# Axial attention: values and embeddings summed into one PSUM tile of 32-row strips

## Chip, cores and metric

The kernel runs on one core of one Trainium2 chip. The metric is the device time of a whole execution in microseconds (us). The kernel before takes 5311.62 us as the median of three runs (5309.52 to 5312.31).

## What is computed

The program is four residual layers on an image `x` of 2 x 128 x 128 x 128 (batch, channels, height, width), all in float32: an axial attention, four directional scans, a deformable convolution and a transformed convolution. Only the first layer is touched:

```python
x = x + L0(group_norm(x))
# L0: for every image n, column w and group g of 8, over the 128 rows h
q, k (8 x 128), v (16 x 128) = batch_norm(w_qkv applied to x)
qr = einsum('bgci,cij->bgij', q, q_emb)
kr = einsum('bgci,cij->bgij', k, k_emb).swapaxes(2, 3)
qk = einsum('bgci,bgcj->bgij', q, k)
sim = softmax(sum of batch_norm([qk, qr, kr]), axis=3)
sv  = einsum('bgij,bgcj->bgci', sim, v)        # the values
sve = einsum('bgij,cij->bgci', sim, v_emb)     # the embeddings
out = batch_norm(concat([sv, sve])) summed over the two
```

The last batch norm needs the mean and variance of every channel of `sv` and of `sve` over all images and columns.

## The kernel before

`layer0_prepare` writes the scaled q and k (scratch tensors `qa`, `qb`) and the values (`v`) to DRAM. `layer0_attention` (from line 615) does the rest, and `Merge` (line 931) reads `sv` and `sve` back, normalises them with the statistics and adds them to the image.

**Units and pairs.** Line 669 lists 64 units: image `n`, then group `g`, then a block `wc` of 32 columns. A unit has four *pairs* of 8 columns each, so there are 256 pairs. The loop at line 867 runs over pairs `m`, and then 15 rounds more to drain. The engines are wrapped in `InOrder` (line 75): every engine executes its instructions in the order in which the loop writes them, so this order is the schedule. Line 83 is the helper's line, and nearly everything in the profile bears it; groups are told apart by their tiles.

**One round m**, in order:

1. `logits_pe` (line 726): 8 transposes of the position term `r` and 8 small products of q and k add up in the PSUM tile `lg`; `add_term` (VectorE) adds the other term into `e`.
2. `turn`/`turned` for pair m-2: TensorE transposes half of the finished `e` into PSUM `te`, VectorE copies it to `et`.
3. `maxima` of pair m (VectorE), `divide` of pair m-1 (VectorE's reciprocal of `total`, then POOL's multiplication of `e`).
4. `values` for pair m-3 (line 804): 8 products `et` x `v` into `po`, each into 16 rows of one of four 32-row strips; ScalarE copies `po` to `svt`.
5. `terms_pe` for the next unit: 16 products into the PSUM tile `gen`; `terms_copy`: three quarters by ScalarE, one quarter by VectorE, into `r`.
6. `embedded_pe` for piece m-7 (line 819): 32 products `et2` x `ve`, again into 16 rows of four strips of the same `po`; ScalarE copies `po` to `ste`.
7. the second half of the transposes, then POOL's `by_position`, which rearranges `et` into `et2`; last the 8 `exponentials` of pair m on ScalarE, with their sums.
8. `stats` (line 848, called from line 906): one `bn_stats` over 512 elements for each half unit of `svt` and of `ste`, so four per unit; a `bn_aggr` when a group is complete.
9. the loads on SyncE's queue (SP) for units to come: 16 of `zz` and one of `vt` (line 684, three buffers), four of `qk`; then the stores of `svt` and `ste`, four each.

Both products use the one PSUM tile `po` (line 657), one after the other, with a ScalarE copy after each. Each float32 product shows in the profile as two records of weight load and matmul, a transpose as one.

At the start of the attention the table `ve` is loaded by ScalarE's queue (line 650) and `zz` is cleared by POOL (line 655). At the end, `Merge.scales` (line 970) gathers the statistics with one small matmul (line 982) through a constant matrix `gather` (line 2107).

Of the kernel before, what the change touches and what calls it, by code (L numbers as in the profile page):

```python
# [7 lines left out]
F32 = mybir.dt.float32  # L8
I32 = mybir.dt.int32
AF = mybir.ActivationFunctionType  # L10
ALU = mybir.AluOpType
# [4 lines left out]
P = 128  # L16
N = 2
S = 128
RT = 4
NT = S // RT  # L20
WC = 32
NC = S // WC
NB = S // 16
NG = 8
# [589 lines left out]
def layer0_attention(env, prm, mem, alphas, mv, then):  # L614
# [14 lines left out]
    nc, tc = env.nc, env.tc  # L629
    pe, dve, act, pool, sync = (  # L630
        InOrder(tc, e) for e in (nc.tensor, nc.vector, nc.scalar, nc.gpsimd, nc.sync)
    )
    ident = env.ident
    HW = WC // 2
    with ExitStack() as ctx:
        early = ctx.enter_context(ExitStack())
        cp = ctx.enter_context(tc.tile_pool(name="at_c", bufs=1))
# [7 lines left out]
        st_v, st_e = (  # L645
            cp.tile([P, NG, N * NC, 2, 6], F32, name=f"st_so{k}", tag=f"st_so{k}")
            for k in range(2)
        )
# [25 lines left out]
        def load(at):  # L674
            u = Unit()
            u.n, u.g, u.wc = units[at]
            u.z = zz[at % 2]
            u.base = 64 * (at % 2)
            for i in range(16):
                sync.dma_start(  # L680
                    out=u.z[8 * i : 8 * i + 8, :, i % 4].rearrange("p t b w -> p t (b w)"),
                    in_=qb[u.g, u.n, u.wc, i],
                )
            u.v = sp.tile([P, WC, 16], F32, name="vt", tag="vt", bufs=3)
            sync.dma_start(out=u.v, in_=mem["v"][u.g, u.n, u.wc])
            u.r = {}
            return u

# [115 lines left out]
        def values(u, p, et):  # L804

            for r in range(2):
                for x in range(RT):
                    pe.matmul(
                        po_v[32 * x : 32 * x + 16, r, :],
                        lhsT=u.v[:, (2 * p + r) * RT + x, :],  # L810
                        rhs=et[:, r * RT + x, :],
                        start=True,
                        stop=True,
                    )
            if p == 0:
                u.sv = sp.tile([P, 2 * RT, S], F32, name="svt", tag="svt")
            act.copy(u.sv[:, 2 * p : 2 * p + 2, :], po_v)

        def embedded_pe(u, k):
# [12 lines left out]
        def embedded_copy(u, k):  # L832
            if k == 0:
                u.sve = sp.tile([P, WC, WC], F32, name="ste", tag="ste")
            act.copy(u.sve[:, 8 * k : 8 * k + 8, :], po_e)

        def store_sv(u):
            for x in range(4):
                sync.dma_start(out=sv[u.g, x, :, u.n, u.wc], in_=u.sv[32 * x : 32 * x + 16])

        def store_sve(u):
            for s in range(4):
                sync.dma_start(
                    out=sve[u.g, s, :, u.n, u.wc],
                    in_=u.sve[32 * s : 32 * s + 16].rearrange("p i w -> p (i w)"),
                )

        def stats(u, st, t, half):
            dve.bn_stats(
                st[:, u.g, u.n * NC + u.wc, half, :],  # L850
                t.rearrange("p a b -> p (a b)")[:, 512 * half : 512 * half + 512],
            )

        pairs = 4 * len(units)
        us, es, ets, totals = {}, {}, {}, {}
        for at in range(2):
            us[at] = load(at)  # L860
            load_qk(us[at])
        for t in range(2):
            for k in range(2):
                ps = terms_pe(us[0], t, k)
                for s in (0, 1):
                    terms_copy(us[0], t, k, ps, s)
        for m in range(pairs + 15):
            here = m < pairs
            if m == pairs:
                early.close()  # L870
# [24 lines left out]
            if 0 <= piece < pairs:  # L895
                embedded_pe(us[piece // 4], piece % 4)
                embedded_copy(us[piece // 4], piece % 4)
            if turning:
                te = turn(e, 1)
                turned(et, 1, te)  # L900
                by_position(ub, pb, et)
                ets[m - 2] = et
            if here:
                totals[m] = exponentials(es[m], mx)

            for st, k, half in ((st_v, 7, 0), (st_v, 8, 1), (st_e, 11, 0), (st_e, 14, 1)):
                if m >= k and (m - k) % 4 == 0 and (m - k) // 4 < len(units):
                    done = us[(m - k) // 4]
                    stats(done, st, done.sv if st is st_v else done.sve, half)
                    if half == 1 and done.n == N - 1 and done.wc == NC - 1:  # L910
                        k = int(st is st_e)
                        every = st[:, done.g].rearrange("p e f k -> p (e f k)")
                        dve.bn_aggr(mv[:, done.g, k, :], every)
# [4 lines left out]
            if m % 4 == 3 and m >= 7 and (m - 7) // 4 < len(units):  # L918
                store_sv(us[(m - 7) // 4])
            if m % 4 == 3 and m >= 11 and (m - 11) // 4 < len(units):  # L920
                store_sve(us[(m - 11) // 4])
            if m % 4 == 2 and m >= 14 and (m - 14) // 4 < len(units):
                us.pop((m - 14) // 4)

# [6 lines left out]
class Merge:  # L931
# [38 lines left out]
    def scales(self, cp, pp, prm, mv):  # L970
# [5 lines left out]
        gather = cp.tile([P, P + NG], F32, name="gather", tag="gather")  # L976
        nc.scalar.dma_start(out=gather, in_=prm["cst"][:, 8 * P : 9 * P + NG])
# [4 lines left out]
        nc.tensor.matmul(  # L982
            ps.rearrange("p g k -> p (g k)"),
            lhsT=gather[:, 0:P],
            rhs=mv.rearrange("p g k m -> p (g k m)"),
            start=True,
            stop=True,
        )
        own = cp.tile([P, NG, 4], F32, name="own", tag="own")
        nc.vector.tensor_tensor(  # L990
            own, ps, gather[:, P : P + NG].unsqueeze(2).to_broadcast([P, NG, 4]), ALU.mult
        )
        gm = cp.tile([P, 2, 2], F32, name="gm_out", tag="gm_out")
        nc.vector.tensor_reduce(
# [1097 lines left out]
def constants(np):  # L2092

    k, m = np.arange(P)[:, None], np.arange(P)[None, :]
    ident = k == m
# [8 lines left out]
    ones = k >= 0 * m  # L2104


    gather = (k % 32 == m % 16) * 0.25
    own = k // 16 == m
    parts = [ident, group_avg, strip, *sel, *selv, ones, gather, own]
# [110 lines left out]
```

## Time and profile before

| what | value |
|---|---|
| median of 3 runs | 5311.62 us |
| profiled execution | 5305.85 us |
| its span | 5304.1 us |
| TensorE busy (matmuls, whole span) | 4974.9 us, 94% |
| VectorE, ScalarE, POOL busy | 3521.7, 2658.8, 2126.1 us |
| first gen matmul of the attention | 402.9 us |
| last copy of po | 1923.9 us |
| `svt<-po` copies on ScalarE | 256, median 0.358 us |
| `ste<-po` copies on ScalarE | 256, median 0.364 us |
| `po<-et,vt` and `po<-et,ve` matmul records | 4096 and 16384 |
| DMA packets, mean rate | 499988, 66 GB/s |

A row of the timeline gives the start, the time from the first start to the last end, the engine, the line, the operation with its tiles (written <- read), the shapes and how many instructions are merged. PE is TensorE's matmuls, PEld its weight loads, DVE VectorE, ACT ScalarE, SP the queue of SyncE. A bracket says how long the engine was idle before, and what ended it. Matmuls are pipelined, so the start of one group to the start of the next is a better measure than the duration. In a list of waits the numbers are the total in us, how many, and the longest.

### The profile page before, as it was taken

How to read it: one execution, taken by the hardware profiler on the slowest of the kernel's cores; microseconds unless marked ns; L12 is line 12 of the kernel's file. 1: busy time of each engine (PE TensorE's matmuls, PEld its weight loads, DVE VectorE, ACT ScalarE, POOL GpSimd, SP SyncE). 2: the span in 40 equal slices, each digit the busy share in tenths (PEclk: the TensorE clock that was granted, in tenths of full speed). 3: DMA queues.
4: the chain of work that ended last, by engine and by line, in shares of the span. 5: the costliest groups of instructions: out<-in, count | busy, mean ns of one | idle time of the engine just before them, and what ended most of it. 6: DMA issues, size and time to landing. Idle time of an engine off the chain costs nothing. (4 is left out here: it accounts for less than half of the span.)

```text
span 5304.1 us, 179050 instructions
## 1 busy us (share of the span) xinstructions
PE 4974.9 (94%) x76283; PEld 4306.7 (81%) x76283; DVE 3521.7 (66%) x6818; ACT 2658.8 (50%) x7718; POOL 2126.1 (40%) x1749
## 2 busy tenths in 40 slices
PE   7898999999999934999999999999989999999999
PEld 6767888888888834999999999998468888888777
DVE  3636888888888857555555555666346666666688
ACT  3557898888889845554222332001334443443322
POOL 3214666666666634000000000333035555555576
PEclk8998999999999966999999999999989999999999
DMA  4362333333333369970000000101321111111011
GB/s 160 122 252 63 62 62 61 58 61 62 59 59 63 61 258 305 92 65 2 1 1 1 1 1 1 49 33 38 117 69 35 35 33 38 33 33 32 35 53 57
DMA packets 499988, 347.61 MB, mean 66 GB/s; under 512 B 311669, under 2 KB 456565, under 8 KB 487281
## 3 DMA queue, kind: packets, MB, share of 16 engines
q1 hardware_dynamic: 494144, 326.50, 27.0%
q8 instruction: 607, 9.95, 0.8%
q10 hardware_dynamic: 5040, 9.56, 0.5%
q14 instruction: 197, 1.61, 0.1%
HBM read 194.99 MB, written 157.72 MB: 66 GB/s over the span
## 5 line engine op out<-in xcount | busy, mean ns | idle before, releaser
L83 PE MATMUL pl<-ln,wl 128*128 128x128 f32 (+1 forms) x10160 | 1241.2, 276 | 9.3 <-DVE ln L83 7.8
L83 PEld LDWEIGHTS pl<-ln,wl 128*128 128x128 f32 x10160 | 1176.1, 190 | 22.3 <-issue 6.7
L83 POOL TENSOR_TENSOR w<-d 128x504 f32<-128x504 f32 x512 | 558.6, 1115 | 669.4 <-DVE s L83 612.8
L83 ACT ACTIVATE e<-e,mx 128x128 f32<-128x128 f32 x2048 | 793.4, 395 | 0.8 <-DVE mx L83 0.8
L83 POOL TENSOR_TENSOR res<-ln,x1t 128x128 f32<-128x128 f32 x256 | 149.3, 584 | 1428.2 <-DVE ln L83 1428.2
L83 POOL TENSOR_TENSOR e<-e,total 128x1024 f32<-128x1024 f32 x256 | 485.9, 1898 | 486.4 <-DVE total L83 477.1
L83 ACT COPY res<-ln 128x64 f32<-128x64 f32 (+1 forms) x1016 | 283.9, 304 | 702.2 <-DVE ln L83 702.2
L83 ACT COPY sm<-ps_s 128x1152 f32<-128x1152 f32 x256 | 286.6, 1119 | 562.6 <-PE ps_s L83 562.6
L83 PE MATMUL po<-sm,wdef 128*128 128x256 f32 x2304 | 567.5, 392 | 0.0
L83 PEld LDWEIGHTS ps_s<-s,xw 28*128 28x128 f32 x10240 | 456.6, 187 | 122.2 <-issue 77.2
L83 PE MATMUL pl<-ln,ws 128*128 128x128 f32 x4064 | 536.8, 273 | 0.0
L83 PE MATMUL ps_s<-s,xw 28*128 28x240 f32 (+2 forms) x10240 | 520.0, 343 | 16.4 <-DMA xw<-px_d 13.9
L83 POOL COPY et<-et 128x1024 f32<-128x1024 f32 x256 | 516.4, 2017 | 35.2 <-DVE et L83 27.0
L83 DVE TENSOR_TENSOR v<-pl,c 128x128 f32<-128x128 f32 x508 | 148.1, 291 | 540.7 <-PE pl L83 537.4
L83 PEld LDWEIGHTS pl<-ln,ws 128*128 128x128 f32 x4064 | 494.5, 190 | 0.0
L83 ACT ACTIVATE r<-gen,alphas 128x1536 f32<-128x1536 f32 x256 | 395.0, 1543 | 170.6 <-PE gen L83 143.6
L83 PEld LDWEIGHTS po<-sm,wdef 128*128 128x128 f32 x2304 | 418.4, 190 | 71.0 <-issue 0.2
L83 ACT ACTIVATION_READ_ACCUMULATOR e<-e,mx 128x1 f32 x2048 | 396.5, 194 | 0.0
L83 DVE SCALAR_TENSOR_TENSOR ln<-v,res 128x128 f32<-128x128 f32 x1016 | 347.0, 342 | 48.5 <-POOL res L83 0.9
L83 DVE STREAM_TRANSPOSE s<-w 128x1152 f32<-128x1152 f32 x256 | 349.8, 1367 | 33.0 <-PE ps_s L83 29.9
L83 PE MATMUL te<-cst_main,e 128*128 128x128 f32 x2048 | 338.5, 287 | 28.7 <-POOL e L83 20.9
L83 DVE COPY et<-te 128x512 f32<-128x512 f32 x512 | 348.2, 680 | 12.9 <-PE te L83 12.4
(246 smaller groups left out, 8405.5 us busy)
## 6 DMA issues: line engine op xcount, KB each, us to landing
xw<-px_d SPq DMA_DIRECT2D x528, 56.0 KB
xa<-in_x SPq DMA_DIRECT2D x16, 1024.0 KB
v_d<-vs SPq DMA_DIRECT2D x16, 1024.0 KB
qb_d<-sb SPq DMA_DIRECT2D x16, 1024.0 KB
qa_d<-sa SPq DMA_DIRECT2D x8, 2048.0 KB
zz<-qb_d SPq DMA_DIRECT2D x1024, 16.0 KB
vt<-v_d SPq DMA_DIRECT2D x64, 256.0 KB
qk<-qa_d SPq DMA_DIRECT2D x256, 64.0 KB
```

Source lines behind the costliest of these rows:

```text
L83: return lambda *a, **k: self.tc.keep_in_program_order(issue(*a, **k))
```

## The change

`values` and `embedded_pe` no longer write `po` one after the other; they add into it. Each strip of 32 rows holds the values of pair m-3 in rows 0 to 15 and the embeddings of piece m-7, which belongs to the unit before, in rows 16 to 31. For this the weights are 32 columns wide: `vt` is now three fixed tiles with zeros in the upper 16 columns (set once), and `ve` has zeros in the lower 16. The values start the sum, the embeddings add onto it (in the last rounds, where there are no values, the embeddings start it). One ScalarE copy `both_copy` takes `po` to a tile `so`, and one `bn_stats` per half unit covers both, so two per unit.

The units are ordered by group first, so that the eight entries of a group lie one after the other in the statistics, values at entry b and embeddings at entry b+1. The stores take rows 0 to 15 and 16 to 31 of each strip of `so` and alternate between `sv` and `sve`. The loop drains in 8 rounds. The constant `gather` has two matrices, and `scales` two matmuls.

```diff
-        ve = cp.tile([P, S, 16], F32, name="ve", tag="ve")
-        nc.scalar.dma_start(out=ve, in_=prm["vemb"])
+        ve = cp.tile([P, S, 32], F32, name="ve", tag="ve")
+        nc.gpsimd.memset(ve[:, :, 0:16], 0.0)
+        nc.scalar.dma_start(out=ve[:, :, 16:32], in_=prm["vemb"])
+        vt = [cp.tile([P, WC, 32], F32, name=f"vt{j}", tag=f"vt{j}") for j in range(3)]
+        for t in vt:
+            nc.gpsimd.memset(t[:, :, 16:32], 0.0)
...
-        units = [(n, g, wc) for n in range(N) for g in range(NG) for wc in range(NC)]
+        units = [(n, g, wc) for g in range(NG) for n in range(N) for wc in range(NC)]
...
-            u.v = sp.tile([P, WC, 16], F32, name="vt", tag="vt", bufs=3)
-            sync.dma_start(out=u.v, in_=mem["v"][u.g, u.n, u.wc])
+            u.v = vt[at % 3]
+            sync.dma_start(out=u.v[:, :, 0:16], in_=mem["v"][u.g, u.n, u.wc])
...
-                        po_v[32 * x : 32 * x + 16, r, :],
+                        po_v[32 * x : 32 * x + 32, r, :],
                         lhsT=u.v[:, (2 * p + r) * RT + x, :],
                         rhs=et[:, r * RT + x, :],
-                        start=True,
-                        stop=True,
+                        start=(r == 0),
+                        stop=False,
...
-            act.copy(u.sv[:, 2 * p : 2 * p + 2, :], po_v)
...
-                        po_e[32 * s : 32 * s + 16, i % 8, :],
+                        po_e[32 * s : 32 * s + 32, i % 8, :],
                         lhsT=ve[:, at, :],
                         rhs=u.et[:, at, :],
-                        start=True,
-                        stop=True,
+                        start=(alone and i % 8 == 0),
+                        stop=(i % 8 == 7),
...
-            act.copy(u.sve[:, 8 * k : 8 * k + 8, :], po_e)
+        def both_copy(b, k):
+
+            if k == 0:
+                sos[b] = sp.tile([P, 4, 256], F32, name="so", tag="so")
+            act.copy(sos[b][:, k, :], po)
...
-        for m in range(pairs + 15):
+        for m in range(pairs + 8):
...
-            for st, k, half in ((st_v, 7, 0), (st_v, 8, 1), (st_e, 11, 0), (st_e, 14, 1)):
+            for k, half in ((5, 0), (7, 1)):
...
-        nc.tensor.matmul(
-            ps.rearrange("p g k -> p (g k)"),
-            lhsT=gather[:, 0:P],
...
+        for k in range(2):
+            nc.tensor.matmul(
+                ps[:, :, 2 * k : 2 * k + 2],
+                lhsT=gather[:, k * P : (k + 1) * P],
```

More of the change, by code (lines that the diff above doesn't have):

```diff
@@ L643, in layer0_attention @@
         pp = ctx.enter_context(tc.tile_pool(name="at_ps", bufs=1, space=PSUM))
[L645 to L648, printed above, removed]
-        ve = cp.tile([P, S, 16], F32, name="ve", tag="ve")
-        nc.scalar.dma_start(out=ve, in_=prm["vemb"])
+        st = cp.tile([P, NG * N * NC + 1, 2, 6], F32, name="st_so", tag="st_so")
+        ve = cp.tile([P, S, 32], F32, name="ve", tag="ve")
[4 more added lines that the diff above has]
+            nc.gpsimd.memset(t[:, :, 16:32], 0.0)
         toep = zp.tile([P, 2, 8, S], F32, name="toep", tag="toep")
@@ L808, in values, with embedded_pe @@
                     pe.matmul(
-                        po_v[32 * x : 32 * x + 16, r, :],
+                        po_v[32 * x : 32 * x + 32, r, :],
                         lhsT=u.v[:, (2 * p + r) * RT + x, :],
                         rhs=et[:, r * RT + x, :],
-                        start=True,
-                        stop=True,
-                    )
-            if p == 0:
-                u.sv = sp.tile([P, 2 * RT, S], F32, name="svt", tag="svt")
-            act.copy(u.sv[:, 2 * p : 2 * p + 2, :], po_v)
-        def embedded_pe(u, k):
+                        start=(r == 0),
+                        stop=False,
+                        skip_group_check=True,
+                    )
+        def embedded_pe(u, k, alone):
             for i in range(8 * k, 8 * k + 8):
@@ L824, in embedded_pe @@
                     pe.matmul(
-                        po_e[32 * s : 32 * s + 16, i % 8, :],
+                        po_e[32 * s : 32 * s + 32, i % 8, :],
                         lhsT=ve[:, at, :],
                         rhs=u.et[:, at, :],
-                        start=True,
-                        stop=True,
+                        start=(alone and i % 8 == 0),
+                        stop=(i % 8 == 7),
+                        skip_group_check=True,
                     )
-        def embedded_copy(u, k):
+        def both_copy(b, k):
@@ L833, in embedded_copy, with store @@
             if k == 0:
-                u.sve = sp.tile([P, WC, WC], F32, name="ste", tag="ste")
-            act.copy(u.sve[:, 8 * k : 8 * k + 8, :], po_e)
-        def store_sv(u):
+                sos[b] = sp.tile([P, 4, 256], F32, name="so", tag="so")
+            act.copy(sos[b][:, k, :], po)
+        def store(b, so):
             for x in range(4):
[L839 to L846, printed above, removed]
@@ L848, in stats @@
-        def stats(u, st, t, half):
+                if b < len(units):
+                    u = us[b]
+                    sync.dma_start(
+                        out=sv[u.g, x, :, u.n, u.wc],
+                        in_=so[32 * x : 32 * x + 16].rearrange("p k (r h) -> p (k r) h", r=2),
+                    )
+                if b > 0:
+                    u = us[b - 1]
+                    sync.dma_start(
+                        out=sve[u.g, x, :, u.n, u.wc],
+                        in_=so[32 * x + 16 : 32 * x + 32].rearrange("p k i -> p (k i)"),
+                    )
@@ L849, in stats @@
+        def stats(b, half):
             dve.bn_stats(
-                st[:, u.g, u.n * NC + u.wc, half, :],
-                t.rearrange("p a b -> p (a b)")[:, 512 * half : 512 * half + 512],
-            )
+                st[:, b, half, :],
+                sos[b].rearrange("p k i -> p (k i)")[:, 512 * half : 512 * half + 512],
+            )
+            per = N * NC
+            for k in range(2):
+                g, rest = divmod(b + 1 - k, per)
+                if half == 1 and rest == 0 and g > 0:
+                    g -= 1
+                    every = st[:, per * g + k : per * g + k + per]
+                    dve.bn_aggr(mv[:, g, k, :], every.rearrange("p e f k -> p (e f k)"))
@@ L857, in layer0_attention @@
         pairs = 4 * len(units)
-        us, es, ets, totals = {}, {}, {}, {}
+        us, es, ets, totals, sos = {}, {}, {}, {}, {}
         for at in range(2):
@@ L895, in layer0_attention @@
             if 0 <= piece < pairs:
-                embedded_pe(us[piece // 4], piece % 4)
-                embedded_copy(us[piece // 4], piece % 4)
+                embedded_pe(us[piece // 4], piece % 4, m - 3 >= pairs)
+            if m >= 3:
+                both_copy((m - 3) // 4, (m - 3) % 4)
             if turning:
@@ L904, in layer0_attention @@
                 totals[m] = exponentials(es[m], mx)
-            for st, k, half in ((st_v, 7, 0), (st_v, 8, 1), (st_e, 11, 0), (st_e, 14, 1)):
[L907 to L913, printed above, removed]
+            for k, half in ((5, 0), (7, 1)):
+                if m >= k and (m - k) % 4 == 0:
+                    stats((m - k) // 4, half)
             if m % 4 == 3 and m // 4 + 2 < len(units):
@@ L917, in layer0_attention @@
                 load_qk(us[m // 4 + 1])
[L918 to L921, printed above, removed]
+            if m % 4 == 3 and m >= 7:
+                store((m - 7) // 4, sos.pop((m - 7) // 4))
             if m % 4 == 2 and m >= 14 and (m - 14) // 4 < len(units):
@@ L975, in scales @@
         nc.scalar.dma_start(out=vec, in_=prm["vecout"])
-        gather = cp.tile([P, P + NG], F32, name="gather", tag="gather")
-        nc.scalar.dma_start(out=gather, in_=prm["cst"][:, 8 * P : 9 * P + NG])
+        gather = cp.tile([P, 2 * P + NG], F32, name="gather", tag="gather")
+        nc.scalar.dma_start(out=gather, in_=prm["cst"][:, 8 * P : 10 * P + NG])
         sq = cp.tile([P, NG, 2], F32, name="sq_out", tag="sq_out")
@@ L981, in scales @@
         ps = pp.tile([P, NG, 4], F32, name="ps_mv", tag="ps_mv")
-        nc.tensor.matmul(
-            ps.rearrange("p g k -> p (g k)"),
-            lhsT=gather[:, 0:P],
[L985 to L988, printed above, removed]
+        for k in range(2):
+            nc.tensor.matmul(
+                ps[:, :, 2 * k : 2 * k + 2],
+                lhsT=gather[:, k * P : (k + 1) * P],
+                rhs=mv[:, :, k, :],
+                start=True,
+                stop=True,
+            )
         own = cp.tile([P, NG, 4], F32, name="own", tag="own")
         nc.vector.tensor_tensor(
-            own, ps, gather[:, P : P + NG].unsqueeze(2).to_broadcast([P, NG, 4]), ALU.mult
+            own, ps, gather[:, 2 * P : 2 * P + NG].unsqueeze(2).to_broadcast([P, NG, 4]), ALU.mult
         )
@@ L2104, in constants @@
     ones = k >= 0 * m
-    gather = (k % 32 == m % 16) * 0.25
+    gather = [(k % 32 == 16 * t + m % 16) * 0.25 for t in range(2)]
     own = k // 16 == m
-    parts = [ident, group_avg, strip, *sel, *selv, ones, gather, own]
+    parts = [ident, group_avg, strip, *sel, *selv, ones, *gather, own]
     cst = np.concatenate([np.broadcast_to(a, (P, P)).astype(np.float32) for a in parts], 1)
```

## The prediction

> **What bounds the kernel now.** The change touches the attention, which runs from about 403 us to 1925 us of the span, so I asked first who is short of time there, with the busy times of three equal stretches, then for the order of TensorE's work in one pair, then for what TensorE waited for.
>
> ```profile
> core 0: us, PE busy (x) PEld busy (x) DVE busy (x) ACT busy (x) POOL busy (x), PEclk, DMA share, GB/s
> 940.00:1400.00 460.00, 445.55 (x11398) 374.74 (x11396) 394.74 (x560) 410.44 (x1511) 309.63 (x160) 1.00 0.33 61
> ```
>
> TensorE 97%, ScalarE 89%, VectorE 86%, clock 1.00. A busy matmul row is weak evidence, so one pair in order of time:
>
> ```profile
> 1263.30 1.04 PE L83 MATMUL lg<-cst_main,r 128*128 128x128 f32 x8
> 1264.27 1.16 PE L83 MATMUL lg<-qk 8*128 8x128 f32 x16
> 1265.36 0.66 PE L83 MATMUL te<-cst_main,e 128*128 128x128 f32 x4
> 1265.94 0.63 PE L83 MATMUL po<-et,vt 128*16 128x128 f32 x16
> 1266.51 1.17 PE L83 MATMUL gen<-zz,toep 32*128 32x128 f32 x32
> 1267.61 0.73 PE L83 MATMUL po<-et,ve 128*16 128x32 f32 x64
> 1268.27 0.66 PE L83 MATMUL te<-cst_main,e 128*128 128x128 f32 x4
> 1268.76 1.04 PE L83 MATMUL lg<-cst_main,r 128*128 128x128 f32 x8
> ```
>
> From lg to lg is 5.46 us with no idle mark: each group starts where the previous one runs out. Seven groups, from start to start: 0.97 + 1.09 + 0.58 + 0.57 + 1.10 + 0.66 + 0.49 = 5.46. Four pairs make a unit: 21.84 us. The starts of the maxima on VectorE give 23.07 us per unit (from unit 4 to unit 60, 1,292 us over 56). So 1.23 us per unit is TensorE time lost. The waits of its weight loads between 480 and 1860 us name it:
>
> ```profile
> PEld po L83 <- issue: 61.3, 267, 1.4
> PEld gen L83 <- issue: 48.2, 228, 0.2
> PEld te L83 <- POOL e L83: 25.8, 84, 0.7
> PEld te L83 <- issue: 5.6, 16, 1.1
> PEld te L83 <- DVE total L83: 2.3, 2, 1.2
> ```
>
> "Issue" is mostly the normal 0.12 to 0.2 us at each change of group, plus stalls inside a group: the first gen of a unit is some 0.39 us longer (its loads carry the waits on 16 loads of zz), and about one embedded group in eight stops for 0.3 to 1.2 us. The change leaves both. What it can give back is the wait of the transposes te for POOL and VectorE: 25.8 + 2.3 = 28.1 us in 86 waits, of which 0.12 us each is the normal step: 86 × 0.12 = 10.3. Real wait: **17.8 us**. ScalarE, meanwhile, waits 134 us for gen there: it has time to spare.
>
> **The change, part by part.**
>
> **ScalarE.** Per pair one COPY po of 0.36 us goes (256 in all, 92 us busy). On the path it is worth nothing: behind it r waits for gen (0.3 to 0.8 us in nearly every pair), and that wait only grows.
>
> **VectorE.** Four BATCH_NORM_STATS2 of 0.68 us per unit (0.60 from start to start) become two. Where do they decide? A statistic stands ahead of the next pair's sum, copy, maxima and reciprocal; the reciprocal releases POOL's division (1.90 us), which releases te one pair later. From VectorE's r at 1252.30 over two statistics to its r two pairs on, at 1263.86, that chain takes 11.56 us; with one statistic that is 10.96, with none 10.36, against 2 × 5.46 = 10.92 us of TensorE. So one statistic per pair is level with TensorE, two are late. Before, pairs 0 and 2 of a unit end with one, pair 3 with two. The te waits, measured from the end of the qk group to te, fit: about 0.10 us in pair 0, 0.15 in pair 1, 0.04 in pair 2, 0.01 in pair 3 (sum 0.30 per unit). After, pairs 1 and 3 end with one each. Pair 1's wait loses 0.60 us of cause and goes, those of pairs 0 and 2 go; a wait like pair 0's (0 to 0.10) moves to pair 3. The 16 BATCH_NORM_AGGREGATE (0.59) stay 16. Gain between 11.6 us (it moves whole) and 17.8 (all goes). I take **−15**, because TensorE itself becomes a little slower (next part) and so hides more of it.
>
> **TensorE, wider weights.** Every weight load of po goes from 16 columns to 32: 64 records per pair in embedded, 16 in values. Nothing covers this engine, so it counts in full. No row has this operand, but one is near: pg in the stage before, 64 loads of 32 columns in the same four strips.
>
> ```profile
> L83 PEld LDWEIGHTS po<-et,ve x16384: 92/96/132, 466.9 to 1923.6; 128*16 128x16 f32 x200
> L83 PE MATMUL po<-et,ve x16384: 189/193/242, 466.9 to 1923.6; 128*16 128x32 f32 x200
> L83 PEld LDWEIGHTS pg<-zt x2048: 105/109/116, 244.4 to 386.8; 128*32 128x32 f32 x187
> L83 PE MATMUL pg<-zt x2048: 192/197/218, 244.4 to 386.8; 128*32 128x33 f32 x187
> 383.29 0.77 PE L83 MATMUL pg<-zt 128*32 128x33 f32 x64
> ```
>
> One load is 13 ns longer, but the whole group only 0.77 against 0.73 us, a part of that from 33 moving columns in place of 32 (32/33 of 0.77 is 0.75). The Trainium skill (TensorE: Matmul & The Clock Gate, LDWEIGHTS) speaks against this change: load time is the number of columns over 1.2, so 16 more cost 13.3 ns each. The 13 ns in the rows agree; as a sum, an estimate from that page, 64 × 13.3 = 0.85 us per pair or 215 us over 253 pairs. By the group row it is 0 to 0.04, since a load in one strip runs beside matmuls in the others. The row decides: 0.025 per pair. Values stream 128 columns per load: 0. Start and stop flags, and adding onto what lies in po, cost nothing in the lg group, which does the same.
>
> **TensorE, waits.** The first embedded matmul no longer waits for ScalarE. The compiled order shows what comes instead: the last three transposes of the first te carry a wait for ScalarE each (the exponentials two pairs back, long done). In layer 1, weight loads with a satisfied wait are followed by their matmul 111 to 112 ns after the last one, unmarked transposes 109: 3 × 3 ns; as bound 3 × 0.03, the price per wait in the first gen. I take 0.01. Together 0.035 per pair × 253 = **+9** (0 to +30).
>
> **DMA.** The target of vt now lies in pieces of 64 B: 4,096 per unit where there were 128 of 2 KB. The nearest row is x1c_d in layer 1, also 64 B: 32,768 pieces take SP 25.6 us, 1,280 per us, so 3.2 us per unit. The skill (DMA: Bandwidth & Descriptors, Specifications) asks for 512 B and more, below that it sees a read-modify-write; no run here shows one for SBUF, so up to twice that, 6.4 us. Behind vt on SP stand the stores, then qk and zz of later units. SP idles about 8 us ahead of every vt (in one unit from 1027.9 to 1035.9), qk and zz are needed some four pairs later, the DMA share of 0.33 rises to 0.47. Price 0. What is exposed if the cover fails: TensorE's own program arrives by DMA in 16 KB packets of about 1.23 us here, and of about 1.4 in the flood of x1c_d. A unit fetches some four, one in five would meet the flood, and 0.2 us on that one is under 0.2 us per unit even if all of it stalls, while one group in eight stalls now; I take **+1** (0 to +20). The stores keep size and number; values and embeddings alternate and the first copy of an output tile waits for all eight, issued three pairs earlier: 0. The order of units changes which loads come, not how many.
>
> **Start.** Four POOL memsets (16 and 3 × 4 KB) are new; zz's 128x2048 takes 1.81 us, so 4 to 8 us in a POOL that idles 43 us until 433.6. The first vt waits for them on SP, ahead of qk and zz of unit 1. Before, it left at 405.66, 13 us after ve could be loaded. ve in 16,384 pieces takes 12.8 us beside zz's last loads; r on ScalarE comes 17 us after its issue. **+1** (0 to +6).
>
> **Drain.** In the last pairs nothing overlaps: po by values, svt, then embedded 0.49 us after it. Twice that step (0.37 + 0.49, less the 0.2 of a group change) goes: −1.3. The last embedded copy stays last; scales has one small matmul more (0.3). **−1**.
>
> **Sum.** −15 + 9 + 1 + 1 − 1 = −5. The profiled execution was 5305.85 (span 5304.1), 5.8 under the median of 5311.62; its sum gives about 5301, that of the median about 5306.5. I say 5306.
>
> **Rivals.** *Wide loads exposed (slower).* Break-even: 17.8 + 1 us over 253 × 64 = 16,192 loads is 1.2 ns per load. Were strips less independent than in pg, 2 ns per load would be +32 − 15 = +17: 5329. For it: TensorE has no slack. Against: pg shows at most 0.6 ns. 0.18.
> *Fetches late.* The 64 B pieces delay TensorE's program; 0.3 us more stall per unit is +19 over 63 units, 5325. For it: stalls are there already. Against: layer 1's TensorE keeps 99.8% busy through a heavier flood, if with fewer instructions. 0.10, and 0.05 for the start or an aggregate going wrong, near 5324.
> *All te waits go and the wide loads are free.* −17.8 − 1 + 1: 5294. For it: pg's surplus may be its wider operand. 0.22.
> *It only moves waits* belongs to my case: gain 11.6, cost 9, 5309.
>
> **Numbers.** Mine 0.45, with 5299 to 5313. What cannot be told from no change is 0.2%, 10.6 us, so 5301.0 to 5322.2. Faster: 0.08 of mine + 0.20 of the free case = 0.28. Same: 0.37 + 0.02 + 0.01 = 0.40. Slower: 0.17 + 0.10 + 0.05 = 0.32. The range 5294 to 5330 leaves out the tails.
>
> **What will show it.** po<-et,ve ×64 in the timeline at 0.73 to 0.77 us; te waits for POOL under 6 us in all and in pair 3; ScalarE's wait for gen longer by 0.36 per pair; vt's issue near 3 us with no TensorE wait behind it; the unit at 22.9 to 23.0 us. An embedded group of 0.80 or more, or more issue stalls in po, would make the prediction wrong.

## The result, and the profile after

The changed kernel takes **5335.52 us** (median of 8 runs, 5323.03 to 5349.58) against 5311.97 us of the kernel before beside it (8 runs, 5305.67 to 5315.69): ratio 1.0044, 95% interval 1.0031 to 1.0057. It is 23.5 us slower, where 5306 was predicted, and lies above the predicted range of 5294 to 5330. The profiled execution took 5340.66 us (span 5338.4), 34.8 us over the one of before, so the sums below, which come from these two, are larger than the difference of the medians.

What was meant to happen did happen. The waits of TensorE's weight loads between 480 and 1860 us (total us, times, longest), after:

```profile
PEld po L83 <- issue: 65.7, 258, 3.5
PEld lg L83 <- issue: 48.8, 239, 2.3
PEld gen L83 <- issue: 44.7, 220, 0.4
PEld te L83 <- issue: 5.8, 11, 1.1
PEld te L83 <- POOL e L83: 2.8, 8, 0.4
PEld te L83 <- DVE total L83: 1.6, 2, 1.0
```

The wait for POOL fell from 25.8 to 2.8 us. But the longest "issue" of po and lg rose to 3.5 and 2.3 us (1.4 and 0.7 before). One pair in order of time shows the wider weights, 128x32, and almost the old tempo:

```profile
1262.93 0.65 PE L83 MATMUL te<-cst_main,e 128*128 128x128 f32 x4
1263.51 0.65 PE L83 MATMUL po<-et,vt 128*32 128x128 f32 x16
1264.09 1.17 PE L83 MATMUL gen<-zz,toep 32*128 32x128 f32 x32
1265.19 0.76 PE L83 MATMUL po<-et,ve 128*32 128x32 f32 x64
1265.88 0.66 PE L83 MATMUL te<-cst_main,e 128*128 128x128 f32 x4
```

One load of these weights takes 13 ns more, as the rows of the stage before had it:

```profile
L83 PEld LDWEIGHTS po<-et,ve x16384: 106/109/178, 479.7 to 1960.0; 128*32 128x32 f32 x200
```

The loss has two places. The first maxima of the attention come at 439.7 us in place of 427.0: **12.7 us** before the loop has begun. From the first to the last maxima it takes 1494.2 us in place of 1468.5: **25.7 us** in the loop. Of this, 1.6 us comes back by the first load of the next stage.

More than half of the units are as fast as before or faster. A few are not: the first pair of the unit at 1292.9 takes 11.64 us. There TensorE stops in the middle of an embedded group, for 3.42 us:

```profile
1291.97 1.66 PE L83 MATMUL gen<-zz,toep 32*128 32x128 f32 x32
1293.56 0.71 PE L83 MATMUL po<-et,ve 128*32 128x32 f32 x58
1297.69 0.33 PE L83 MATMUL po<-et,ve 128*32 128x32 f32 x6 [3.42 <-issue]
```

What ends it is the arrival of TensorE's own program. The trace lists it as queue q8, "instruction", packets of 16 KB; one comes for every 256 of TensorE's records, matmuls, weight loads and waits on semaphores together (fitted slope 256.0 in both traces). In the trace after, between 480 and 1860 us, 35 intervals between two matmul starts outlast 0.5 us. All but one, a wait of te, end 1.2 to 1.7 us after such a packet has ended. So a stall is a packet that came late. The one above was moved at 1294.42 us, 7.86 us after the one ahead of it, where 5.2 is the mean. Here is what the queues did in between: first the 6.1 us from 1288.2 to 1294.3, then 1294.3 to 1296.2.

```profile
q1 hardware_dynamic: 422, 0.50, 56.3%
q14 instruction: 1, 0.01, 0.8%
issues: line engine op xcount, KB each, median us to landing
qk<-qa_d SPq DMA_DIRECT2D x4, 64.0 KB
zz<-qb_d SPq DMA_DIRECT2D x6, 16.0 KB
```

```profile
q1 hardware_dynamic: 96, 0.07, 28.8%
q8 instruction: 1, 0.02, 5.5%
```

No packet of q8 began until the last of qk's four loads were nearly through. The packet list of this stretch shows qk's pieces of 2 KB in two phases: about half pass at 0.08 us each, the rest, from 1291 us on, at 26 per us and 0.32 us each. 26 x 0.32 = 8.3 engines' time, so some eight engines are full of them. The Trainium skill (DMA: Bandwidth & Descriptors, Why a DMA increments its semaphore by 16 and not by 1) says that a transfer is spread over the largest number of engines up to 16 that divides the slowest dimension of both its sides; that of qk is 8 rows, which agrees.

It is the same at the other long stalls. In all seven of over 1.5 us the late program packet starts between 0.5 us before and 1.0 us after the last packet of qk. It is no rule for every unit, though: between 480 and 1860 us, 35 program packets of the changed kernel start while qk's packets are under way, where an even spread over time would give some 43.

The Trainium skill's page Runtime: NRT & Kernel Launch (Instruction fetch mechanics) calls the fetching of the next 16 KB mostly hidden, since the engine issues more slowly than the fetch fills; here TensorE runs dry for up to 3.6 us, and the measurement decides.

A long stall costs more than its own length, because the clock that TensorE is granted falls beside it. The row of the middle of the attention has 0.98 for the clock (the column PEclk), where the same row of before, in the prediction, has 1.00. Right behind the stall above it is 0.5 for 10.2 us, and the groups take nearly twice their usual 0.66, 1.04 and 1.16 us. First that row, with the columns as in the prediction, then these groups:

```profile
940.00:1400.00 460.00, 445.11 (x11127) 377.59 (x11117) 362.79 (x508) 377.31 (x1387) 301.91 (x155) 0.98 0.40 59
```

```profile
1297.95 1.12 PE L83 MATMUL te<-cst_main,e 128*128 128x128 f32 x4
1298.86 1.91 PE L83 MATMUL lg<-cst_main,r 128*128 128x128 f32 x8
1300.70 2.08 PE L83 MATMUL lg<-qk 8*128 8x128 f32 x16
```

The pair behind, at 1304.6, has no such stall and still takes 7.52 us. Between 480 and 1860 us the changed kernel has seven stretches at 0.5, 41 us in all, and the kernel before has none; six of the seven begin between 0.6 us before and 1.5 us after the end of a stall of over 1.5 us. Apart from stalls, the intervals between matmul starts inside these stretches are about 17 us longer in sum than they are elsewhere.

The pieces of 64 B had long passed when this stall began. SP's queue ahead of that stall (after), and at the like place of before:

```profile
1281.07 0.52 SPq L83 DMA_DIRECT2D vt<-v_d  x1
1284.01 0.32 SPq L83 DMA_DIRECT2D sv_d<-so  x1
...
1288.57 0.43 SPq L83 DMA_DIRECT2D sve_d<-so  x1
1289.09 1.75 SPq L83 DMA_DIRECT2D qk<-qa_d  x4
1290.94 9.32 SPq L83 DMA_DIRECT2D zz<-qb_d  x16
```

```profile
1266.63 0.34 SPq L83 DMA_DIRECT2D vt<-v_d  x1
1267.45 2.25 SPq L83 DMA_DIRECT2D sv_d<-svt  x4
1269.81 1.79 SPq L83 DMA_DIRECT2D sve_d<-ste  x4
1271.69 1.33 SPq L83 DMA_DIRECT2D qk<-qa_d  x4
```

Before, the first store followed vt after 0.8 us and qk after 5.1; now it is 2.9 and 8.0. Between the end of vt's issue and the first store SP stands for 2.4 us in every unit. The first store of values needs the joint copy, which stands behind gen and the embedded products; before, it needed only the copy right behind the values. In the mean qk is issued 19.2 us after the unit's first maxima, and 15.9 us before.

To compare runs, every interval between matmul starts was set against the usual one of its place in the pair (the 20% point), between 480 and 1860 us, and scaled to 253 pairs. "Usual pair" is the sum of the usual intervals, "te" the waits of te behind qk, "gen" the excess in gen (the first of a unit waits for its loads), "program" all other excess, the slow clock's as well as the stalls'. Of the change in us per pair, 5.772 to 5.880, this accounts for nearly all:

| | before | after | x 253 |
|---|---|---|---|
| usual pair | 5.451 | 5.494 | +10.9 us |
| te | 0.074 | 0.021 | -13.5 us |
| gen | 0.097 | 0.114 | +4.2 us |
| program | 0.141 | 0.246 | +26.5 us |

The 17 us of the slow clock lie in the last two rows: about 13 in program and 5 in gen, which is all of gen's growth. So of the 31 us in these rows somewhat over half came with the slow clock, the rest with the late packets themselves.

### The profile page after: what moved, and what is told of

Its sections match the earlier page's. It is cut to its first block, busy times and chain, and to the rows that moved or that the text cites. A ratio compares the mean times of both kernels' runs of the same rounds, so it can differ in the third digit from the quotient of the medians.

```text
span 5338.4 us, 178548 instructions
## 1 busy us (share of the span) xinstructions
PE 4996.5 (94%) x76285; PEld 4338.0 (81%) x76285; DVE 3452.3 (65%) x6692; ACT 2587.9 (48%) x7467; POOL 2133.2 (40%) x1753
## 3 DMA queue, kind: packets, MB, share of 16 engines
q1 hardware_dynamic: 748096, 326.50, 29.1%
## 5 line engine op out<-in xcount | busy, mean ns | idle before, releaser
L83 DVE STREAM_TRANSPOSE s<-w 128x1152 f32<-128x1152 f32 x256 | 349.9, 1367 | 31.8 <-PE ps_s L83 28.8
L83 PE MATMUL gen<-zz,toep 32*128 32x128 f32 x8192 | 337.1, 291 | 35.5 <-DMA zz<-qb_d 27.8
L83 DVE TENSOR_TENSOR e<-lg,r 128x1024 f32<-128x1024 f32 x256 | 310.9, 1215 | 80.3 <-PE lg L83 79.9
## 6 DMA issues: line engine op xcount, KB each, us to landing
vt<-v_d SPq DMA_DIRECT2D x64, 256.0 KB
```

Of the source, the lines that this page charges most:

```text
L83: return lambda *a, **k: self.tc.keep_in_program_order(issue(*a, **k))
```

## The experiments

Theory A: the pieces of 64 B hold up TensorE's program (my rival "fetches late"). Theory S: the stores' later wait moves the loads of qk to a place in the unit where the program is due, and the pieces matter little. Theory W: the wider weights. The first four kernels are edits of the kernel before; all are compared with runs of the kernel before beside them. A difference in us is the ratio less one, times the median of those runs; the plain medians differ from it by up to 4 us (b_late 17.8 in place of 13.8, a_both 33.7 in place of 36.6). "Te" and "program" are us over 253 pairs, "over 1.5" counts program stalls of more than 1.5 us between 480 and 1860 us, "qk issued" is the mean in us after the first maxima of the unit, "clock 0.5" the us of that window, up to the last maxima, at a granted clock of 0.5. All columns but the ratio come from one profiled execution each, which need not be typical: that of b_spread is 9 us and that of a_emb1 12 us under the median of its runs, that of a_padve 11 us over it. The first maxima differ by up to 5 us between kernels with the same start.

| kernel | ratio to before (95%) | usual pair | te | program | over 1.5 | clock 0.5 | qk issued | first maxima |
|---|---|---|---|---|---|---|---|---|
| before | | 5.451 | 18.7 | 35.8 | 0 | 0 | 15.9 | 427.0 |
| after | 1.0044 (1.0031 to 1.0057) | 5.494 | 5.2 | 62.3 | 7 | 41.0 | 19.2 | 439.7 |
| b_spread | 0.9983 (0.9975 to 0.9991) | 5.451 | 12.5 | 33.6 | 0 | 0 | 16.2 | 424.2 |
| b_vt64 | 1.0031 (1.0019 to 1.0043) | 5.456 | 18.7 | 60.7 | 8 | 27.3 | 18.5 | 420.8 |
| b_wide | 1.0000 (0.9991 to 1.0008) | 5.482 | 15.6 | 33.2 | 1 | 6.8 | 15.9 | 423.6 |
| b_late | 1.0026 (1.0015 to 1.0037) | 5.456 | 18.8 | 57.7 | 6 | 34.1 | 18.2 | 427.5 |
| a_vt16 | 0.9949 (0.9936 to 0.9963) | 5.362 | 1.0 | 49.8 | 7 | 17.1 | 17.8 | 440.1 |
| a_padve | 1.0030 (1.0019 to 1.0040) | 5.496 | 5.3 | 57.7 | 7 | 41.0 | 19.1 | 432.4 |
| a_order | 1.0015 (1.0008 to 1.0022) | 5.496 | 4.6 | 29.3 | 1 | 0 | 15.2 | 437.5 |
| a_both | 0.9931 (0.9917 to 0.9944) | 5.352 | 2.0 | 52.6 | 6 | 27.3 | 17.8 | 432.4 |
| a_noqk | 1.0003 (0.9993 to 1.0012) | 5.496 | 4.5 | 29.1 | 0 | 0 | none | 438.1 |
| c_order | 0.9901 (0.9885 to 0.9918) | 5.341 | 2.5 | 30.6 | 1 | 0 | 14.9 | 429.1 |
| c_ve | 0.9896 (0.9879 to 0.9912) | 5.341 | 2.7 | 29.9 | 0 | 3.4 | 14.9 | 423.3 |
| a_emb1 | 0.9952 (0.9938 to 0.9966) | 5.351 | 2.3 | 36.4 | 4 | 0 | 14.8 | 442.4 |

**b_spread: one statistic per pair, nothing else.**

```diff
-            for st, k, half in ((st_v, 7, 0), (st_v, 8, 1), (st_e, 11, 0), (st_e, 14, 1)):
+            for st, k, half in ((st_v, 7, 0), (st_v, 8, 1), (st_e, 13, 0), (st_e, 14, 1)):
```

> The kernel before, with only the first statistic of the embeddings moved from pair 3 of a unit (which had two) to pair 1, so that one follows the copies in pairs 0, 1, 2 and 3. Removes nothing else. If the transposes' waits for POOL come from two statistics standing in one pair (my prediction's part on VectorE), the waits of te for POOL and VectorE between 480 and 1860 us fall from 28 us to under 14, and the time by some 5 to 12 us, since one statistic per pair is still level with TensorE. If only halving the statistics helps, nothing changes: 0 +- 3 us.

Measured: 9.0 us faster (4.8 to 13.3), in the range of the first theory. The wait behind qk falls by 6.2 us, yet not as the expectation had it: the profile's own waits hardly move.

```profile
PEld te L83 <- POOL e L83: 23.4, 112, 0.7
PEld te L83 <- DVE total L83: 1.9, 2, 1.2
```

There are more of them, 112 in place of 84, and they are smaller; less the normal 0.12 us of each, 25.3 - 13.7 = 11.6 us remain of 17.8. So about a third of the wait was the two statistics in one pair; the rest went only where there were fewer statistics, as in the changed kernel.

**b_vt64: only the pieces of 64 B.**

```diff
-            u.v = sp.tile([P, WC, 16], F32, name="vt", tag="vt", bufs=3)
-            sync.dma_start(out=u.v, in_=mem["v"][u.g, u.n, u.wc])
+            u.v = sp.tile([P, WC, 32], F32, name="vt", tag="vt", bufs=3)
+            sync.dma_start(out=u.v[:, :, 0:16], in_=mem["v"][u.g, u.n, u.wc])
...
-                        lhsT=u.v[:, (2 * p + r) * RT + x, :],
+                        lhsT=u.v[:, (2 * p + r) * RT + x, 0:16],
```

> The kernel before, with the tile vt 32 columns wide and loaded into its lower 16 columns, so in pieces of 64 B as in the changed kernel; the products still read 16 columns, and all else is as before. Theory A (the small pieces delay TensorE's program, which then stalls): the stalls inside TensorE's groups grow as in the changed kernel, outlying pairs of 7 to 11 us appear after the load, +15 to +27 us. Theory S (the stores' later wait on SP moves the qk and zz loads to where the program is due, and the pieces do nothing): 0 to +4 us. Theory W (it is all in the wider weights): 0.

Measured: 16.5 us slower, the long stalls are there: as Theory A has it. But SP shows that this edit, too, moves qk. The eight stores behind vt take 3.62 + 3.28 us where they took 2.25 + 1.79, and qk leaves 2.6 us later in the unit:

```profile
1262.49 0.52 SPq L83 DMA_DIRECT2D vt<-v_d  x1
1263.29 3.62 SPq L83 DMA_DIRECT2D sv_d<-svt  x4
1267.01 3.28 SPq L83 DMA_DIRECT2D sve_d<-ste  x4
1270.38 1.35 SPq L83 DMA_DIRECT2D qk<-qa_d  x4
```

Why the stores take longer behind the pieces no run shows. So this run alone does not tell A from S.

**b_wide: only the wider weights of the embedded products.** Each load takes the next row's 16 columns too; what they give is never used. (`ve` gets one more row for this, cleared once by VectorE.)

```diff
-                        po_e[32 * s : 32 * s + 16, i % 8, :],
-                        lhsT=ve[:, at, :],
+                        po_e[32 * s : 32 * s + 32, i % 8, :],
+                        lhsT=ve[:, at : at + 2, :].rearrange("p a b -> p (a b)"),
```

> The kernel before, with the weights of the embedded products 32 columns wide: each takes the next row's 16 columns as its upper half, and the result's upper 16 rows are never read. No DMA, wait, copy or statistic changes. Theory W: the embedded group is 31 ns longer from first to last start (0.568 against 0.537 us), 253 pairs make +8 us; part of that is hidden by the waits for POOL that it shortens, so +4 to +8 us, with no new stalls above 2 us. If wider weights also cost something between groups, more than +10.

Measured: no difference (-4.8 to +4.2 us). The usual pair is 31 ns longer as expected, 7.8 us in all; the waits of te shorten by 3.1 us and the program's by 2.6. Theory W can't carry 23 us; the values' wider weights are not in this run, but they add only 0.013 us per pair, 3.3 us in all, to the usual pair of the changed kernel.

**b_late: the stores exchanged, so that the first waits for the later copy.**

```diff
+            if m % 4 == 3 and m >= 11 and (m - 11) // 4 < len(units):
+                store_sve(us[(m - 11) // 4])
             if m % 4 == 3 and m >= 7 and (m - 7) // 4 < len(units):
                 store_sv(us[(m - 7) // 4])
-            if m % 4 == 3 and m >= 11 and (m - 11) // 4 < len(units):
-                store_sve(us[(m - 11) // 4])
```

> The kernel before, with the two groups of stores on SP exchanged: first the four of the embeddings, then the four of the values. The first of them then waits for the copy behind the embedded products, as in the changed kernel, so the loads of qk and zz behind it are issued some 2 us later in the unit. Theory S: TensorE's stalls grow, +8 to +25 us. Theory A: 0 to +3 us.

Measured: 13.8 us slower, with six stalls over 1.5 us, and vt still in whole rows. No byte, no piece and no instruction differs, only SP's order:

```profile
1267.52 0.34 SPq L83 DMA_DIRECT2D vt<-v_d  x1
1270.46 1.71 SPq L83 DMA_DIRECT2D sve_d<-ste  x4
1272.21 2.97 SPq L83 DMA_DIRECT2D sv_d<-svt  x4
1275.28 1.32 SPq L83 DMA_DIRECT2D qk<-qa_d  x4
```

The gap of 2.6 us behind vt is the wait for the copy, and qk leaves 7.8 us after vt in place of 5.1. The clock of 0.5 is there too, 34 us of it. Theory S.

**a_vt16: vt narrow and in whole rows again, the embedded products first.** From here on the kernels are edits of the changed one.

```diff
-            if 0 <= m - 3 < pairs:
-                values(us[(m - 3) // 4], (m - 3) % 4, ets.pop(m - 3))
...
                 embedded_pe(us[piece // 4], piece % 4, m - 3 >= pairs)
+            if 0 <= m - 3 < pairs:
+                values(us[(m - 3) // 4], (m - 3) % 4, ets.pop(m - 3), piece < 0)
```

with `start=(i % 8 == 0)` in the embedded products, `start=(alone and r == 0)` and 16 rows in the values, and vt loaded as before the change.

> The changed kernel, with vt 16 columns wide again and loaded in whole 2 KB rows. So that values need no zeros, the embedded products come first and start the sum (32 rows, zeros in the lower 16), and the values, moved behind gen and embedded, add 16 rows onto it. Weights of values are narrow again (14 ns per pair, 3.5 us in all). Theory A: no outlying pairs of 7 to 11 us, TensorE's stalls back at those of before, 22 to 30 us faster than the changed kernel, so within -8 to +2 us of the kernel before. Theory S: the stores still wait for the copy, so only the 3.5 us are gained, +18 to +22 us against before.

Measured: 27.0 us faster than before. Neither theory gave that. Theory A's core fails: without any pieces of 64 B in the loop seven stalls over 1.5 us stand, with qk at 17.8. The program's excess is 12.5 us smaller than in the changed kernel, though; this run changes too much at once to tell why. Most of the surplus comes from elsewhere: the usual pair fell from 5.494 to 5.362 us, 33 us over 253 pairs, and gen's excess from 28.8 to 15.2. a_emb1 takes up the first.

**a_padve: ve sent with its zeros, whole rows.** The table of 32 columns, zeros included, is made on the host.

```diff
-        nc.gpsimd.memset(ve[:, :, 0:16], 0.0)
-        nc.scalar.dma_start(out=ve[:, :, 16:32], in_=prm["vemb"])
+        nc.scalar.dma_start(out=ve, in_=prm["vemb"])
```

> The changed kernel, with the table of the embeddings sent with its 16 zero columns, so that it arrives as one load in 16 KB rows and POOL clears nothing for it. If the pieces of 64 B of ve held up the first zz loads, the first maximum comes at 427 to 429 us in place of 439.7 and the whole is 10 to 13 us faster than the changed kernel: +9 to +14 us against before. If POOL's clearing did it, much the same time is gained but with the load of zz as slow as before; if neither, +22 to +26 us.

Measured: 15.9 us slower than before (10 to 21), a little more than the +9 to +14 expected, and the first maxima at 432.4, not at 427 to 429. The start, in SP's queue and TensorE's first gen: the changed kernel's two lines, then this kernel's, then before's.

```profile
387.21 31.11 SPq L83 DMA_DIRECT2D zz<-qb_d  x16
418.42 0.76 PE L83 MATMUL gen<-zz,toep 32*128 32x128 f32 x2 [16.16 <-DMA zz<-qb_d]
```

```profile
387.74 22.27 SPq L83 DMA_DIRECT2D zz<-qb_d  x16
```

```profile
388.21 17.40 SPq L83 DMA_DIRECT2D zz<-qb_d  x16
```

The pieces of ve do hold the first zz, by 31.1 - 22.3 = 8.8 us. The other 4.9 us stay. A likely cause is the load's double size, 2 MB in place of 1 MB: in c_ve below, where ve's load goes later, the first zz take 15.0 us.

**a_order: the stores one pair later in SP's order, behind qk.** Pieces of 64 B and wide values stay. (The stores of the drain, which would be left over, follow in the last round.)

```diff
-            if m % 4 == 3 and m >= 7:
-                store((m - 7) // 4, sos.pop((m - 7) // 4))
+            if m % 4 == 0 and m >= 8:
+                store((m - 8) // 4, sos.pop((m - 8) // 4))
```

> The changed kernel, with the eight stores one pair later in SP's order, behind the qk loads in place of ahead of them. Theory S: qk no longer stands behind the wait for the copy, stalls fall, 10 to 20 us faster than the changed kernel. Theory A: the pieces still come just ahead of qk, no gain of more than 4 us: +20 to +26 us against before.

Measured: +8.0 us against before, so some 15 faster than the changed kernel. The program's excess is smaller than before the change, 29.3 us, and the clock stays at 1.00 from 480 to 1860 us. TensorE's waits at its matmuls, this kernel and then the changed one:

```profile
PE po L83 <- issue: 13.5, 21, 1.5
PE lg L83 <- issue: 2.4, 5, 0.8
```

```profile
PE po L83 <- issue: 23.0, 22, 3.4
PE lg L83 <- issue: 7.2, 8, 2.0
```

This decides between A and S in the main: with the 4,096 pieces per unit in place, the long stalls are gone when qk leaves early. A small part for the pieces is not excluded. a_emb1, which has them, shows four stalls of over 1.5 us and 36.4 us of program, and c_order, with qk at the same place but no pieces and narrow values, one stall and 30.6.

**a_both: both repairs.** The edits of a_vt16 and a_padve together:

```diff
-            u.v = vt[at % 3]
-            sync.dma_start(out=u.v[:, :, 0:16], in_=mem["v"][u.g, u.n, u.wc])
+            u.v = sp.tile([P, WC, 16], F32, name="vt", tag="vt", bufs=3)
+            sync.dma_start(out=u.v, in_=mem["v"][u.g, u.n, u.wc])
...
-        nc.scalar.dma_start(out=ve[:, :, 16:32], in_=prm["vemb"])
+        nc.scalar.dma_start(out=ve, in_=prm["vemb"])
...
```

> The changed kernel with both repairs: vt loaded in 2 KB rows with the embedded products first, and ve sent with its zeros. Theory A: the start of before and its stalls, the waits for POOL gone (-13 us), the embedded weights wide (+8 us): -4 to -14 us against before. Theory S: +6 to +10.

Measured: 36.6 us faster than before, beyond both, for the reason of a_vt16. Six long stalls remain, with 27 us at a clock of 0.5.

**a_noqk: no loads of qk after the second unit.** The later units multiply old q and k.

```diff
-            if m >= 4 and m % 4 == 0 and m // 4 + 1 < len(units):
-                load_qk(us[m // 4 + 1])
```

> The changed kernel with the loads of qk left out after the first two units, so that later units multiply old q and k: the logits are not those of the reference. Everything else, the pieces of 64 B and the stores' wait too, stays. If TensorE's program waits behind the packets of qk (26 a us, 0.32 us each, on some eight of the engines), the long pairs of 7 to 11 us go, and the stalls outside gen and te's first wait fall from 0.25 us per pair to under 0.12: 20 to 35 us faster than the changed kernel, so -12 to +3 us against before. If the pieces or the loads of zz hold the program, the long pairs stay: +15 to +24 us.

Measured: +1.6 us against before, 22 faster than the changed kernel, no stall over 1.5 us, program 29.1 us. With the loads of zz, the stores and the pieces all there, the long stalls go with qk alone. (The loads behind it on SP come earlier, too, so the run by itself does not tell qk's packets from their place. For the packets speaks that all seven late program packets of the changed kernel start as qk's end.)

```profile
PE po L83 <- issue: 15.2, 24, 1.0
PE lg L83 <- issue: 1.5, 4, 0.5
```

**c_order: both repairs and the stores behind qk.** The edits of a_both, and that of a_order:

```diff
-            if m % 4 == 3 and m >= 7:
+            if m % 4 == 0 and m >= 8:
```

> Both repairs (vt in 2 KB rows with the embedded products first, ve sent with its zeros) and the stores behind the qk loads. The run with both repairs still had five pairs of 9 to 11 us where 5.4 is normal, all in units whose qk was issued 17 to 19 us after the unit's first maxima. With qk at 15 to 16 us they should go, 15 to 25 us more: -50 to -62 us against before. If these stalls don't hang on where qk is issued, no gain: -33 to -39.

Measured: 52.5 us faster than before, with qk at 14.9 us, one stall of 1.7 us left and no slow clock in the loop, as expected.

**c_ve: that, and ve loaded in the first round of the loop.**

```diff
-        nc.scalar.dma_start(out=ve, in_=prm["vemb"])
...
+            if m == 0:
+                act.dma_start(out=ve, in_=prm["vemb"])
```

> As the run with both repairs and the stores behind qk, and the load of ve issued by ScalarE at the end of the first round of the loop in place of ahead of toep. It is first read seven rounds later. If its 2 MB stand before toep and zz at the start, the first maxima come at 418 to 426 us in place of 432.4, so 6 to 12 us faster than that run. If not, the same within 3 us.

Measured: 55.2 us faster than before, median 5249.33 us, but not to be told from c_order. The first zz take 15.0 us of SP in place of 20.5 and the first maxima come 5.8 us earlier; the loop is 2.7 us longer. A gain in the whole time is not shown: 5.8 us is little more than such starts differ by themselves.

**a_emb1: a_order with the embedded products first**, values still wide and vt in pieces of 64 B.

```diff
-            if 0 <= m - 3 < pairs:
-                values(us[(m - 3) // 4], (m - 3) % 4, ets.pop(m - 3))
...
+            if 0 <= m - 3 < pairs:
+                values(us[(m - 3) // 4], (m - 3) % 4, ets.pop(m - 3), piece < 0)
```

with the start and stop flags of a_vt16.

> The run with the stores behind qk (pieces of 64 B and wide values kept), with one more edit: the embedded products start the sum and the values, moved behind them, add onto it. In the two runs with both repairs the values follow the embedded products with no step between the groups (0.01 us in place of 0.12 to 0.20), so a pair takes 5.37 us in place of 5.50. If that step is the surplus of these runs over what was expected of them, this edit alone gives 0.13 us x 253 = 30 to 34 us over the run with the stores behind qk: -20 to -28 us against before. If the surplus came from the narrow values or the whole rows of vt, 0 to 5 us: +3 to +8 against before.

Measured: 25.5 us faster than before, so 33 from this edit. A pair of a_both shows where it comes from (the profile splits the two groups where their matmuls interleave; a pair of a_emb1 has the same steps):

```profile
1241.37 0.73 PE L83 MATMUL po<-et,ve 128*32 128x32 f32 x62
1241.91 0.27 PE L83 MATMUL po<-et,vt 128*16 128x128 f32 x1
1241.92 0.20 PE L83 MATMUL po<-et,ve 128*32 128x32 f32 x1
...
1242.50 0.66 PE L83 MATMUL te<-cst_main,e 128*128 128x128 f32 x4
```

The values start 0.54 us after the embedded products, in among their last ones. Everywhere else a change of group costs 0.11 to 0.20 us from start to start. A pair loses one step: 5.35 in place of 5.50. Why these two groups run on as one is not shown. That both add into the same tile can't be enough: the two groups of lg do so too, and 0.20 us lie between them.

## Why the prediction was wrong, step by step

**VectorE and the waits of te (-15): right.** 13.5 us went, between the two ends given; b_spread shows that the two statistics of pair 3 were a part of the cause and their number the rest.

**ScalarE (nothing): right.** Its wait for gen grew from 134 to 223 us, and TensorE's weight loads waited for ScalarE once, for 0.3 us. (VectorE waited longer for ScalarE's part of r, 197 us in place of 161, off TensorE's path.)

**TensorE's wider weights (+9): right in kind.** +10.9 by the usual pair: the embedded group from 0.537 to 0.567 us, more than the 0.025 taken and within the 0 to 0.04 of the row, and 0.013 for the values, where I had written 0. The three te waits on ScalarE showed no cost. The group row decided rightly: the 13 ns per load of the rule in the Trainium skill (TensorE: Matmul & The Clock Gate, LDWEIGHTS) are there, but 64 of them add up to 0.03 us, not 0.85 (the estimate made from that page).

**DMA and TensorE's program (0 + 1, range 0 to 20): this step failed.** It measured +26.5 us in program and +4.2 in gen. The sentence that failed is that of the copy of an output tile: I asked who must wait for the stores, found nobody, and wrote 0. I did not ask what the stores themselves now wait for. Their source is the joint copy, behind the embedded products; SP, which issued in the order of the loop in every row here, stands 2.4 us, and qk behind it leaves 3.3 us later in the unit (b_late, by itself, 13.8 us). And I set the program's packets against the 64 B flood only, at 0.2 us each, not against the qk loads, which were there before. The pieces themselves were priced too high: vt's issue took SP 0.52 us, not about 3, and the pieces passed in some 2.5 us, where I had allowed 3.2 to 6.4. The program's packets took 1.13 us each in the loop before, in the mean, not 1.23.

**The clock (no term): missed.** The prediction read a granted clock of 1.00 and carried it into the changed kernel. Beside the long stalls it fell to 0.5, and about 17 of the 31 us above came that way.

Theory S was not among my rivals; "fetches late" had the right victim, with the pieces in place of qk as the culprit. Its 5325 is nearer to the result than my 5306, but by luck in part: it holds neither the clock nor the start. Of my signs, the embedded group (0.76 us), the waits of te for POOL (2.8 us) and ScalarE's longer wait came as written, the unit of 22.9 to 23.0 us did not (it took 23.5), and one of the two signs of being wrong did: issue stalls in po grew, the longest from 1.4 to 3.5 us.

**The start (+1, range 0 to 6): failed by size.** It cost 12.7 us, in one execution of each. I had counted 12.8 us for ve's pieces "beside zz's last loads". But TensorE's first gen was waiting for just those loads, so what lay beside them was the path.

**The drain (-1): right**, 1.6 us.

Sum: -13.5 + 10.9 + 26.5 + 4.2 + 12.7 - 1.6 = +39 us, against 34.8 between the profiled executions; the loop by its maxima is 25.7 us longer, by this sum 28.1.

**What stays open.** Why just an issue of qk at 17.8 to 19.2 us in the unit is bad and one at 14.8 to 16.2 is not (a_emb1 has four stalls there, the longest 2.0 us, where the others at that place have none or one up to 1.7, and those at 17.8 and later reach 3.3 to 3.9). A guess: 256 records make a program packet, and of the 288 matmuls and weight loads of a pair 128 lie in the 0.6 us of the embedded group, so many packets come due there, and one due at the start of qk's transfer waits longest. By the count of records a packet comes up to about 5 us late after the change and 3 before, but also about 4 in a_noqk, where nothing stalls for long. This was not tried by itself. Open too are why the clock falls beside some stalls and not beside others of the same length (none at 1471.6 us, behind one of 2.3 us), and why gen's excess halves when gen follows te directly.

## What to carry to other kernels

When two results are merged into one tile, ask for every reader of the old tiles what it waits for now, stores included, and what is queued behind it: here a wait of 2.4 us in SP's queue, which held up no data that an engine was waiting for, cost about as much as the change gave (13.8 us in b_late, against 13.5 from the waits of te). An engine's own program is a transfer as well; here it came late as the loads into eight rows ended, so it is worth a look where such loads stand. And when an engine stalls for microseconds, read the granted clock behind the stall: here it took as much again. Last, an accumulation into one tile frees the order: more came of putting the two groups behind each other (33 us) than of the copies and statistics saved.

## What the runs showed that was not expected

- The 2 KB packets of qk, into 8 rows at a time, passed in two phases: in the traces before and after, 40% took about 0.08 us each, the others about 0.3 us, 26 per us. Those of vt before, into 128 rows, went up to 109 per us, most at 0.08 us.
- Beside a stall of 1.5 to 3.6 us of TensorE the granted clock fell to 0.5 for 3.4 to 10.2 us, in six cases of seven.
- In the trace after, TensorE goes on 1.2 to 1.7 us after a program packet has ended, whatever the length of the stall.
- Two matmul groups of different weights and widths that add into the same strips follow each other without the step of 0.11 to 0.20 us seen between all other groups.
- A table of 1 MB in 16,384 pieces of 64 B held up 16 loads of 16 KB on another queue, when they were the ones waited for: 31.1 us, against 22.3 with twice the bytes in whole rows.
